# Column sums of a non-local attention block, computed from two exact halves against ones, and a group's end cut into ten pieces

## The chip, the cores and the metric

The kernel runs on one core of a Trainium2 chip. The metric is device time in microseconds (us) of one execution. Five engines run their own instruction streams in program order: PE (TensorE: weight loads and matmuls), ACT (ScalarE), DVE (VectorE), POOL (GpSimd) and SP (SyncE). Here POOL and SP mostly issue DMAs. An instruction whose operands are not ready holds up everything behind it on its engine, DMA issues included.

## The reference

```python
# x: (4, 64, 64, 256); Wq, Wk: 256 x 128; Wv: 256 x 256; N = 64 * 64
q = jnp.einsum('bwhc,cd->bwhd', x, Wq) + bq
k = jnp.einsum('bwhc,cd->bwhd', x, Wk) + bk
v = jnp.einsum('bwhc,cd->bwhd', x, Wv) + bv
pq = q.reshape(B, -1, N)
pk = k.reshape(B, -1, N)
pv = v.reshape(B, -1, N)
energy = jnp.einsum('bcn,bcm->bnm', pq, pk)
attention = jax.nn.softmax(energy, axis=-1)
out = jnp.einsum('bcm,bnm->bcn', pv, attention)
return gamma * out.reshape(B, W, H, C) + x
```

Everything is float32.

## The kernel before

**Tiling.** There are 4 images. For each, a projection stage of 16 iterations makes q, k and v; then attention runs 8 groups (g) of 512 columns n, and each group 16 steps (t) of 256 rows m. A step is counted through the image as u = 16 g + t, so an image has 128 steps. In a step the energies of two blocks of 128 rows are computed, exponentiated to a tile x of 128 x 1024, added to the running sum s, and multiplied by v into four PSUM banks a0, b0, a1, b1 (two halves of the output channels, each with a main bank a and a small-term bank b). No maximum is subtracted; a general version at the end of the program runs only if a sum leaves the safe range.

**Halves.** Matmuls take float32r operands, which keep fewer bits, so each float32 value is split: ACT multiplies it by `UPPER = 1 - 2**-13` on its way into a float32r tile (h), and DVE subtracts h from the value (l) and forms a third combination (d). `upper` and `halves` do this for x, `halve_v` for v, `project_qk` for q and k. Attention then needs three kinds of product (`attend`, line 364), the energies also three (`cross` line 307, `energy` line 322).

**Order of the work.** The schedule is written by hand: the program's order is each engine's order. Within step u PE runs the small-term energies of step u+3, the first half of the attention products of step u, the main energies of step u+2, and the second half of the products. ACT scales the small-term energies (line 308), exponentiates step u+2 (line 325) and makes its upper half (line 331). DVE works on step u+1: adds x to s (line 340), makes l (line 345) and d (line 347). In the last step of a group (t = 15) DVE also adds the two halves of s (line 351), one step ahead, and ACT empties the four banks into o (line 378).

**Buffers.** k tiles are loaded from DRAM by POOL (`load_k`, line 295), u+5 in step u; the pool `kpool` has five buffers. At the start of an image `begin` loads the tiles of steps 0 to 4 in iterations 4 to 8 of the projection stage, the q tile of group 0 in iteration 6, and computes the first energies: the small-term ones of steps 0, 1 and 2 in iterations 10, 11 and 13, the main ones of steps 0 and 1 in iterations 11 and 13. The tile f, through which q and k halves go out to DRAM on POOL's queue (kf at line 263, qd twice at line 265), has two buffers. Projection iteration i transposes x of iteration i+1 (line 122), and loads x of iteration i+2 on SP's queue (line 82; three buffers). Its four PSUM tiles in rotation are the output banks from iteration 3 on.

**A group's end.** After the last products of a group, `finish` starts; it is a Python generator, whose pieces are run one per step by `proceed`, or one per iteration of the next projection stage if the group was the image's last. Its first piece runs at once:

1. `sums`: four float32 matmuls, each with 128 columns of s (every fourth) as weights and one column of ones as moving operand, give the column sums on partitions (line 386); ACT copies 128 x 4 numbers (line 393).
2. Reciprocal (line 396); it is written to DRAM `rd` (line 398) and read back spread over all partitions as r (line 400); o's two parts are added (line 401). In the first seven groups of an image the DMAs go on SP's queue, in the last group on POOL's.
3. and 4. Nothing.
5. o times r (line 405).
6. A DMA on POOL accumulates x onto o (line 409), and o goes out (line 410).

The very last group of the program has its own end, `finish_last`.

Of the kernel before, what the change touches and what calls it, by code (L numbers as in the profile page):

```python
# [9 lines left out]
F32 = mybir.dt.float32  # L10
F32R = mybir.dt.float32r
I32 = mybir.dt.int32
AF = mybir.ActivationFunctionType
ALU = mybir.AluOpType
# [6 lines left out]
def kernel(  # L21
# [62 lines left out]

    ident = const.tile([P, P], F32, name="ident")
    make_identity(nc, ident)
    ones = const.tile([P, P], F32, name="ones")
    nc.vector.memset(ones, 1.0)
    wqk_sb = const.tile([P, KC, 2 * C2], F32, name="wqk_sb")
    bqk_sb = const.tile([P, 2 * C2], F32, name="bqk_sb")  # L90
    nc.gpsimd.dma_start(bqk_sb[:, :C2], bq.partition_broadcast(P))
# [106 lines left out]
    with ExitStack() as fast:  # L198
# [4 lines left out]
        xpool, xtpool, qkv = pool("xpool", 3), pool("xtpool", 3), pool("qkv", 1)  # L203
        ppool = pool("ppool", 2)
        work = pool("work", 2)
        kpool = pool("kpool", 5)
        dram = pool("dram", 2, space=DRAM)
        ps_e = pool("ps_e", 4, space=PSUM)
        ps_o = pool("ps_o", 1, space=PSUM)
# [2 lines left out]
        vh, vl, vd = (  # L212
            qkv.tile([P, NM, C], F32R, tag=name, name=name) for name in ("vh", "vl", "vd")
        )
        rd = dram.tile([B * NG, NB], F32, tag="rd", name="rd", bufs=1)
        nc.scalar.dma_start(wqk_sb[:, :, :C2], wq.rearrange("(k p) d -> p k d", p=P))
        nc.scalar.dma_start(wqk_sb[:, :, C2:], wk.rearrange("(k p) d -> p k d", p=P))

# [115 lines left out]
        def halves(b, u):  # L334
            if u >= STEPS:
                return
            x, h = units[b, u]
            if u % NU:
                s = now["s"]
                nc.vector.tensor_tensor(s, s, x, ALU.add)  # L340
            else:
                now["s"] = x
            ld = ppool.tile([P, 2, 2, NB], F32R, tag="ld", name=f"ld_{b}_{u}")
            l, d = ld[:, 0], ld[:, 1]
            nc.vector.tensor_tensor(l, x, h.bitcast(F32), ALU.subtract)  # L345

            nc.vector.scalar_tensor_tensor(  # L347
                d, h.bitcast(F32), 1.0 + E, x, ALU.mult, ALU.subtract
            )
            if u % NU == NU - 1:  # L350
                nc.vector.tensor_tensor(s[:, 0, :], s[:, 0, :], s[:, 1, :], ALU.add)
                now["sum"] = s[:, 0, :]
            units[b, u] = h, l, d

        def attend(b, u, j, order=(0, 1, 2)):
# [23 lines left out]
                    now["o"][:, c, j, :], now["ab"[c], j], AF.Identity, scale=scale  # L379
                )  # L380

        def sums(b, g, pool, tag):

            zp = pool.tile([P, NJ], F32, tag=tag, name=f"z_{b}_{g}")
            for j in range(NJ):
                nc.tensor.matmul(  # L386
                    zp[:, j : j + 1], now["sum"][:, j::NJ], ones[:, :1], start=True, stop=True
                )
            return zp, rall[:, b * NG + g, :]

        def finish(b, g, o):
            zp, r4 = sums(b, g, ps_o, "b0")
            nc.scalar.copy(r4, zp)
            queue = nc.sync if g < NG - 1 else nc.gpsimd
            yield
            nc.vector.reciprocal(r4, r4)
            n = b * NG + g
            queue.dma_start(rd[n : n + 1, :].rearrange("o (p j) -> (o p) j", j=NJ), r4)
            r = work.tile([P, NB], F32, tag="r", name=f"r_{b}_{g}", bufs=1)
            queue.dma_start(r, rd[n, :].partition_broadcast(P))  # L400
            nc.vector.tensor_tensor(o[:, 0], o[:, 0], o[:, 1], ALU.add)
            yield
            yield
            yield
            nc.vector.tensor_tensor(
                o[:, 0], o[:, 0], r.unsqueeze(1).to_broadcast([P, 2, NB]), ALU.mult
            )
            yield
            nc.gpsimd.dma_start(o[:, 0], xg[b, g], accum_op=ALU.add)
            queue.dma_start(og[b, g], o[:, 0])  # L410

        def inside(ok, r):

# [3 lines left out]
        def finish_last(b, u, xr):  # L417

            g = NG - 1
            attend(b, u, 0)  # L420
            zp, r4 = sums(b, g, ps_e, "e")
            nc.vector.reciprocal(r4, zp)
            work_ = ppool.tile([P, 2, NB], F32, tag="x", name="last", bufs=3)
            spread, ok = work_[:, 0].rearrange("p (q j) -> p q j", j=NJ), work_[:, 1, : B * NG * NJ]
            nc.vector.tensor_tensor(  # L425
                spread,
                ident.unsqueeze(2).to_broadcast([P, P, NJ]),
                r4.unsqueeze(1).to_broadcast([P, P, NJ]),
                ALU.mult,
            )  # L430
            inside(ok, rall.rearrange("p n j -> p (n j)"))
            nc.vector.tensor_reduce(zs, ok, AX.X, ALU.min)
            emptied(b, g, 0)
            o = now["o"]
            attend(b, u, 1, (2,))
            rp = ps_e.tile([P, NB], F32, tag="e", name="rp")
            nc.tensor.matmul(rp, ones, work_[:, 0], start=True, stop=True)  # L437
            attend(b, u, 1, (0, 1))
            np_ = ps_e.tile([P, 1], F32, tag="e", name="np")
            nc.tensor.matmul(np_, ones, zs, start=True, stop=True)  # L440
            nc.scalar.activation(o[:, 1, 1, :], now["b", 1], AF.Identity, scale=gam)
            r = work.tile([P, NB], F32, tag="r", name="r_last", bufs=1)
            nc.scalar.copy(r, rp)
            nc.vector.tensor_tensor(o[:, 0, 0, :], o[:, 0, 0, :], o[:, 1, 0, :], ALU.add)
            nc.vector.tensor_tensor(o[:, 0, 0, :], o[:, 0, 0, :], r, ALU.mult)  # L445
            nc.vector.tensor_tensor(xr[:, 0, :], xr[:, 0, :], o[:, 0, 0, :], ALU.add)  # L446
            nc.sync.dma_start(og[b, g][:, 0], xr[:, 0, :])
            nc.vector.tensor_tensor(o[:, 1, 1, :], o[:, 1, 1, :], r, ALU.mult)  # L448
            nc.vector.tensor_tensor(xr[:, 1, :], xr[:, 1, :], o[:, 1, 1, :], ALU.add)
            nc.vector.scalar_tensor_tensor(o[:, 0, 1, :], now["a", 1], gam1, r, ALU.mult, ALU.mult)  # L450
            nc.vector.tensor_tensor(xr[:, 1, :], xr[:, 1, :], o[:, 0, 1, :], ALU.add)  # L451
            nc.sync.dma_start(og[b, g][:, 1], xr[:, 1, :])
            nc.vector.tensor_scalar(again, np_, P - 0.5, None, ALU.is_lt)
# [15 lines left out]
        for b in range(B):  # L469
            pr = images[b]  # L470
            if b == 0:
                now["banks"] = energies
                pr.transposed(0)

                wp = ps_o.tile([P, P], F32, tag="b1", name="wp1")
                for _ in range(2):
                    nc.tensor.matmul(wp, ones, ones, start=True, stop=True)
                pr.transposed(1)
                project_qk(b, 0)
            for i in range(1, NI):  # L480
                if i == 3:
                    now["banks"] = outputs
                if i + 1 < NI:
                    pr.transposed(i + 1)
                begin(b, i)
                project_qk(b, i)
                if i == NI - 1:
                    halves(b, 0)
                project_v(b, i - 1)
                proceed()  # L490
            project_v(b, NI - 1)
            for u in range(STEPS):
                g, t = divmod(u, NU)
                final = (b, u) == (B - 1, STEPS - 1)
                if t == 6 and g + 1 < NG:
                    load_q(b, g + 1)
                if u == STEPS - NU and b + 1 < B:
                    image(b + 1)
                if u >= STEPS - 3 and b + 1 < B:
                    now["banks"] = energies  # L500
                    if u == STEPS - 3:
                        images[b + 1].load(0)
                    elif u == STEPS - 2:
                        images[b + 1].transposed(0)
                if (b, u) == (B - 1, STEPS - 6):
                    xr = ppool.tile([P, 2, NB], F32, tag="s", name="xr")
                    nc.sync.dma_start(xr, xg[b, g])

                beside = halve_v(b, NI - 2 + u // 4) if u in (2, 6) else iter(())
                cross(b, u + LOOK + 1)  # L510
                if not final:
                    attend(b, u, 0)
                    if t == NU - 1:
                        emptied(b, g, 0)
                energy(b, u + LOOK)
                next(beside, None)
                upper(b, u + LOOK)
                load_k(b, u + LOOK + 3)
                halves(b, u + 1)
                next(beside, None)  # L520
                if final:
                    finish_last(b, u, xr)
                    break
                attend(b, u, 1)
                if t == NU - 1:
                    emptied(b, g, 1)
                    start(finish(b, g, now["o"]))
                else:
                    proceed()
            if b + 1 < B:  # L530
                images[b + 1].transposed(1)
                project_qk(b + 1, 0)
                proceed()
# [134 lines left out]
```

## Time and profile before

| | |
|---|---|
| three runs | 2485.28, 2488.24, 2488.52 us; median 2488.24 |
| the profiled execution | 2489.29 us; its span, first to last instruction, 2487.5 us |
| mean granted TensorE clock | 0.991 |
| busy share: PE, PE weight loads, DVE, ACT, POOL | 98%, 81%, 83%, 74%, 18% |
| matmuls of line 364, 128 x 512 | 6144; mean 390 ns each, overlapping |
| matmuls of line 386 (the sums) | 256 records for 32 groups; 57.6 us busy |
| loads of k (line 295) | 512 of 384 KB; 3.4 us to landing (median) |
| accumulating DMAs (line 409) | 31 of 512 KB; 5.9 us to landing (median) |
| loads of x (line 82) | 64 of 256 KB; 4.4 us to landing (median) |

Matmuls are pipelined, so the duration of one is longer than the time from one start to the next; the time a group costs is read from start to start. A bracket behind an instruction gives the idle time of its engine just before it and what ended it. PEclk is the granted clock, 1 being full speed. POOL's "busy" is the issuing of DMAs.

### The profile page before, as it was taken

Reading aid. Unit: us, or ns where it says so; the run is one execution under the profiler, and the core shown is the slowest. Engines: PE = TensorE matmul, PEld = TensorE weight load, DVE = VectorE, ACT = ScalarE, POOL = GpSimd, SP = SyncE. Lnnn points to the kernel's source line nnn. Section 1 sums busy time; section 2 is a strip of 40 time slices with the busy share of each in tenths; the row PEclk is TensorE's granted clock in tenths of the full one; section 3 lists DMA queues with packets and bytes.
Section 4 is the critical chain, followed back from the end, with each engine's and each line's share of the span. In section 5 each row is a group of like instructions: output and inputs, shape, how many; then the busy total and the mean of one; then the engine's idle time right before and its main releaser. Section 6 shows DMA issues by size and latency. Waiting matters only on the chain. (4 is left out here: it accounts for less than half of the span.)

```text
span 2487.5 us, 30812 instructions
## 1 busy us (share of the span) xinstructions
PE 2428.3 (98%) x10774; PEld 2022.1 (81%) x10774; DVE 2055.8 (83%) x2027; ACT 1832.0 (74%) x3040; POOL 435.6 (18%) x790
## 2 busy tenths in 40 slices
PE   9999999999799999999989999999998999999998
PEld 7788888888688888888868888888886788888886
DVE  5888888888588888888768888888876888888887
ACT  4777777777477777777657777777765777777775
POOL 3211111110321111111032111111113211111110
PEclk9999999999999999999999999999999999999999
DMA  8544444443854444444385444444438444444442
GB/s 250 155 127 127 106 119 131 127 126 95 243 159 126 127 110 114 134 128 121 97 254 153 129 126 127 109 115 135 127 93 257 145 129 130 129 120 118 111 133 74
DMA packets 149779, 338.11 MB, mean 136 GB/s; under 512 B 18641, under 2 KB 51921, under 8 KB 149617
## 3 DMA queue, kind: packets, MB, share of 16 engines
q0 software_dynamic: 115424, 295.89, 42.3%
q1 hardware_dynamic: 33648, 39.91, 5.5%
q8 instruction: 88, 1.44, 0.2%
q14 instruction: 75, 0.61, 0.1%
q10 hardware_dynamic: 544, 0.26, 0.0%
HBM read 268.83 MB, written 67.17 MB: 135 GB/s over the span
## 5 line engine op out<-in xcount | busy, mean ns | idle before, releaser
L325 ACT ACTIVATE x<-e 128x512 f32<-128x512 f32 x960 | 522.3, 597 | 431.3 <-PE e L322 431.2
L340 DVE TENSOR_TENSOR s<-s,x 128x1024 f32<-128x1024 f32 x480 | 587.9, 1225 | 243.9 <-ACT x L325 239.8
L364 PE MATMUL a<-ld,vl 128*128 128x512 f32 x2048 | 631.8, 390 | 6.9 <-DVE ld L345 6.9
L364 PE MATMUL b<-ld,vd 128*128 128x512 f32 x2048 | 632.6, 390 | 1.7 <-DVE ld L347 1.6
L364 PE MATMUL a<-h,vh 128*128 128x512 f32 x2048 | 632.4, 390 | 0.5 <-ACT v L165 0.5
L345 DVE TENSOR_TENSOR ld<-x,h 128x1024 fp32r<-128x1024 f32 x480 | 585.3, 1219 | 2.8 <-DMA qd<-f 2.8
L347 DVE SCALAR_TENSOR_TENSOR ld<-h,x 128x1024 fp32r<-128x1024 f32 x480 | 585.0, 1219 | 0.0
L295 POOL DMA_DIRECT2D k<-kf x512 | 284.2, 556 | 1580.9 <-PE e L322 1456.8
L322 PE MATMUL e<-q,k 128*128 128x512 f32 x2048 | 550.9, 391 | 0.5 <-ACT e L308 0.4
L308 ACT ACTIVATE e<-e 128x512 f32<-128x512 f32 x1024 | 545.0, 566 | 5.0 <-PE e L307 4.9
L331 ACT ACTIVATE h<-x 128x1024 fp32r<-128x1024 f32 x480 | 509.4, 1061 | 15.0
L364 PEld LDWEIGHTS a<-ld,vl 128*128 128x128 f32 x2048 | 384.4, 188 | 88.8 <-DVE ld L345 8.6
L364 PEld LDWEIGHTS b<-ld,vd 128*128 128x128 f32 x2048 | 384.5, 188 | 83.7 <-issue 2.6
L322 PEld LDWEIGHTS e<-q,k 128*128 128x128 f32 x2048 | 385.1, 188 | 81.8 <-ACT e L308 1.5
L364 PEld LDWEIGHTS a<-h,vh 128*128 128x128 f32 x2048 | 384.6, 188 | 81.5 <-ACT v L165 1.2
L307 PE MATMUL e<-q,k 128*128 128x512 f32 x1024 | 319.4, 393 | 0.0
L307 PEld LDWEIGHTS e<-q,k 128*128 128x128 f32 x1024 | 190.6, 189 | 37.4
L260 DVE SCALAR_TENSOR_TENSOR f<-f,qks 128x512 fp32r<-128x512 f32 x128 | 82.8, 689 | 95.3 <-ACT f L258 95.3
L258 ACT ACTIVATE f<-qks 128x512 fp32r<-128x512 f32 x64 | 40.4, 632 | 136.0 <-DVE qks L144 68.6
L135 PE MATMUL qk<-wqk_sb,xts 128*128 128x256 f32 x512 | 131.8, 403 | 3.3 <-ACT xts L128 3.2
L156 PE MATMUL v<-xts,wv_sb 128*128 128x256 f32 x512 | 121.6, 382 | 1.5 <-DVE qks L144 1.5
L135 PEld LDWEIGHTS qk<-wqk_sb,xts 128*128 128x128 f32 x512 | 99.4, 202 | 20.3 <-ACT xts L128 6.5
(67 smaller groups left out, 1093.7 us busy)
## 6 DMA issues: line engine op xcount, KB each, us to landing
k<-kf POOLq DMA_DIRECT2D x512, 384.0 KB, 3.4
kf<-f POOLq DMA_DIRECT2D x64, 384.0 KB, 3.1
qd<-f POOLq DMA_DIRECT2D x128, 192.0 KB, 3.8
q<-qd POOLq DMA_DIRECT2D x32, 768.0 KB, 7.9
x<-in_x_dram SPq DMA_DIRECT2D x64, 256.0 KB, 4.4
o<-in_x_dram POOLq DMA_DIRECT2D x31, 512.0 KB, 5.9
out_dram<-o SPq DMA_DIRECT2D x28, 512.0 KB, 5.5
r<-rd SPq DMA_DIRECT2D x28, 256.0 KB, 4.5
```

What stands on the lines that cost most here:

```text
L135: nc.tensor.matmul(qk[:, s, :], self.xt[i][:, k, s, :], wqk_sb[:, k, :], start=(k == 0), stop=(k == KC - 1),)
L156: nc.tensor.matmul(vp[:, eh, :], wv_sb[:, k, eh * P : (eh + 1) * P], self.xt[i][:, k].rearrange("p s a -> p (s a)"), start=(k == 0), stop= ...
L295: nc.gpsimd.dma_start(t, kf[b, u % NU])
L307: nc.tensor.matmul(e, *forms(b, u, i, 2), start=True, stop=False, skip_group_check=True)
L308: nc.scalar.mul(e, e, -1.0 / (1.0 + E))
L322: nc.tensor.matmul(e, *forms(b, u, i, f), start=False, stop=(f == 1), skip_group_check=True)
L325: nc.scalar.activation(x[:, i, :], e, AF.Exp, scale=(1.0 + E) / E)
L331: nc.scalar.activation(h, units[b, u], AF.Identity, scale=UPPER)
L340: nc.vector.tensor_tensor(s, s, x, ALU.add)
L345: nc.vector.tensor_tensor(l, x, h.bitcast(F32), ALU.subtract)
L347: nc.vector.scalar_tensor_tensor(d, h.bitcast(F32), 1.0 + E, x, ALU.mult, ALU.subtract)
L364: nc.tensor.matmul(to, (vh, vl, vd)[f][:, t + NU * i, j * P : (j + 1) * P], units[b, u][f][:, i, :], start=(t == 0 and i == 0 and f != 1), ...
```

## The change

The sums become two float32r matmuls with a matrix of ones as weights: they stream the upper half and the remainder of s, 512 columns each, and put the column sums on every partition of bank b0. The two halves are made in the group's last step by a new generator, `sum_forms`, one ACT and one DVE instruction, placed between the others of the step. They take the buffer of r, which doubles in size, and `kpool` goes from five buffers to four. The row of sums (one partition) is copied by ACT into the old s tile, written to DRAM `zd`, and read back spread as 128 x 4; from there on the reciprocal, `rd` and r are as before. Each DMA that depends on the one before it is issued a step later, so `finish` has ten pieces: sums and copy; zd written; zd read; reciprocal, rd written and o's parts added; r read; nothing; o times r; accumulation; nothing; output. All DMAs but the accumulation go on SP's queue, in the last group of an image too. The ones are made on DVE from the identity matrix instead of by a memset. The last group of the program keeps its four float32 matmuls.

```diff
-    ones = const.tile([P, P], F32, name="ones")
-    nc.vector.memset(ones, 1.0)
+    ones_r = const.tile([P, P], F32R, name="ones")
+    ones = ones_r.bitcast(F32)
+    nc.vector.tensor_scalar(ones_r, ident, 0.0, 1.0, ALU.mult, ALU.add)
...
-        kpool = pool("kpool", 5)
+        kpool = pool("kpool", 4)
...
-        rd = dram.tile([B * NG, NB], F32, tag="rd", name="rd", bufs=1)
+        zd, rd = (dram.tile([B * NG, NB], F32, tag=n, name=n, bufs=1) for n in ("zd", "rd"))
...
-                now["sum"] = s[:, 0, :]
+                now["sum"] = s
...
-        def sums(b, g, pool, tag):
...
-        def finish(b, g, o):
-            zp, r4 = sums(b, g, ps_o, "b0")
-            nc.scalar.copy(r4, zp)
-            queue = nc.sync if g < NG - 1 else nc.gpsimd
+        def sum_forms(b, g):
+
+            s = now["sum"]
+            f = work.tile([P, 2, NB], F32R, tag="r", name=f"zf_{b}_{g}", bufs=1)
+            h, l = now["z"] = f[:, 0, :], f[:, 1, :]
+            nc.scalar.activation(h, s[:, 0, :], AF.Identity, scale=UPPER)
+            yield
+            nc.vector.tensor_tensor(l, s[:, 0, :], h.bitcast(F32), ALU.subtract)
+            yield
+
+        def finish(b, g, o, s):
+            n = b * NG + g
+            r4 = rall[:, n, :]
+            row = lambda t: t[n : n + 1, :]
+            spread = lambda t: row(t).rearrange("o (p j) -> (o p) j", j=NJ)
+            zp = ps_o.tile([P, NB], F32, tag="b0", name=f"z_{b}_{g}")
+            for f, x in enumerate(now["z"]):
+                nc.tensor.matmul(zp, ones_r, x, start=(f == 0), stop=(f == 1))
+            nc.scalar.copy(s[0:1, 0, :], zp[0:1, :])
+            yield
+            nc.sync.dma_start(row(zd), s[0:1, 0, :])
+            yield
+            nc.sync.dma_start(r4, spread(zd))
             yield
             nc.vector.reciprocal(r4, r4)
-            n = b * NG + g
-            queue.dma_start(rd[n : n + 1, :].rearrange("o (p j) -> (o p) j", j=NJ), r4)
+            nc.sync.dma_start(spread(rd), r4)
+            nc.vector.tensor_tensor(o[:, 0], o[:, 0], o[:, 1], ALU.add)
+            yield
             r = work.tile([P, NB], F32, tag="r", name=f"r_{b}_{g}", bufs=1)
-            queue.dma_start(r, rd[n, :].partition_broadcast(P))
-            nc.vector.tensor_tensor(o[:, 0], o[:, 0], o[:, 1], ALU.add)
-            yield
+            nc.sync.dma_start(r, rd[n, :].partition_broadcast(P))
             yield
             yield
...
             nc.gpsimd.dma_start(o[:, 0], xg[b, g], accum_op=ALU.add)
-            queue.dma_start(og[b, g], o[:, 0])
+            yield
+            yield
+            nc.sync.dma_start(og[b, g], o[:, 0])
...
-                beside = halve_v(b, NI - 2 + u // 4) if u in (2, 6) else iter(())
+                beside = iter(())
+                if u in (2, 6):
+                    beside = halve_v(b, NI - 2 + u // 4)
+                elif t == NU - 1 and not final:
+                    beside = sum_forms(b, g)
+                    total = now["sum"]
```

More of the change, by code (lines that the diff above doesn't have):

```diff
@@ L380, in emptied @@
                 )
-        def sums(b, g, pool, tag):
[L384 to L389, printed above, removed]
-        def finish(b, g, o):
-            zp, r4 = sums(b, g, ps_o, "b0")
-            nc.scalar.copy(r4, zp)
-            queue = nc.sync if g < NG - 1 else nc.gpsimd
+        def sum_forms(b, g):
[19 more added lines that the diff above has]
+            nc.sync.dma_start(r4, spread(zd))
             yield
             nc.vector.reciprocal(r4, r4)
-            n = b * NG + g
-            queue.dma_start(rd[n : n + 1, :].rearrange("o (p j) -> (o p) j", j=NJ), r4)
-            r = work.tile([P, NB], F32, tag="r", name=f"r_{b}_{g}", bufs=1)
-            queue.dma_start(r, rd[n, :].partition_broadcast(P))
+            nc.sync.dma_start(spread(rd), r4)
             nc.vector.tensor_tensor(o[:, 0], o[:, 0], o[:, 1], ALU.add)
             yield
+            r = work.tile([P, NB], F32, tag="r", name=f"r_{b}_{g}", bufs=1)
+            nc.sync.dma_start(r, rd[n, :].partition_broadcast(P))
             yield
@@ L420, in finish_last @@
             attend(b, u, 0)
-            zp, r4 = sums(b, g, ps_e, "e")
+            zp = ps_e.tile([P, NJ], F32, tag="e", name="zp")
+            for j in range(NJ):
+                nc.tensor.matmul(
+                    zp[:, j : j + 1], now["sum"][:, 0, j::NJ], ones[:, :1], start=True, stop=True
+                )
+            r4 = rall[:, B * NG - 1, :]
             nc.vector.reciprocal(r4, zp)
@@ L526 @@
                     emptied(b, g, 1)
-                    start(finish(b, g, now["o"]))
+                    start(finish(b, g, now["o"], total))
                 else:
```

## The prediction

> **What bounds the kernel now.** I read the page first, then the groups by shape, the PE timeline of one group end, the four projection stages, and the waits of POOL and SP.
>
> ```profile
> PE 2428.3 (98%) x10774; PEld 2022.1 (81%) x10774; DVE 2055.8 (83%) x2027; ACT 1832.0 (74%) x3040; POOL 435.6 (18%) x790
> L386 PE MATMUL z<-ones,s 128*128 128x1 f32 x256 | 57.6, 346 | 0.0
> ```
>
> TensorE sets the pace. In a steady step it starts 18 matmuls in 4.08 us (0.227 each), while ACT has 3.4 us and DVE 3.7 us of work in the step. The sums z are 256 records, of which 248 belong to the 31 groups that change. One group end, PE and then ACT:
>
> ```profile
> 2408.40 1.80 PE L386 MATMUL z<-ones,s 128*128 128x1 f32 x8
> 2410.06 0.70 PE L307 MATMUL e<-q,k 128*128 128x512 f32 x2
> 2411.53 0.62 PE L364 MATMUL b<-ld,vd 128*128 128x512 f32 x2
> ...
> 2407.03 1.09 ACT L325 ACTIVATE x<-e 128x512 f32<-128x512 f32 x2
> 2408.15 1.06 ACT L331 ACTIVATE h<-x 128x1024 fp32r<-128x1024 f32 x1
> 2409.68 0.68 ACT L378 ACTIVATE o<-b,gam 128x512 f32<-128x512 f32 x1
> 2410.25 0.16 ACT L393 COPY rall<-z 128x4 f32<-128x4 f32 x1
> ```
>
> PE never idles here: z takes 1.66 us, and a group is 67.07 us where 16 steps are 65.28. ACT is late: it runs without a break from 2404.8, because the four emptyings of the outputs (2.7 us) fall into this step.
>
> The other cost lies in the projection stages. Windows of images 0 to 3 that end at the first attention matmul (those of 1 to 3 start 2.2 us of matmuls earlier in the program; columns: stretch, its length, busy time by engine, clock, DMA share, GB/s):
>
> ```profile
> 12.30:81.20 68.90, 66.16 (x322) 57.43 (x321) 48.68 (x91) 42.84 (x86) 27.03 (x51) 0.98 0.82 250
> 620.30:703.90 83.60, 71.04 (x334) 59.60 (x334) 51.43 (x95) 44.07 (x89) 29.93 (x55) 0.94 0.76 227
> 1241.20:1321.20 80.00, 69.91 (x333) 58.74 (x333) 51.87 (x95) 44.23 (x89) 29.97 (x55) 0.96 0.80 238
> 1858.30:1938.30 80.00, 69.91 (x333) 59.10 (x334) 51.66 (x95) 44.02 (x89) 29.94 (x55) 0.96 0.81 238
> ```
>
> From the same instruction on (the transposition of iteration 1) image 0 takes 68.9 us and the others, less 2.2, take 81.4, 77.8 and 77.8: 30.3 us more in all, and only the others carry a finish of the image before. Its stalls, POOL, ACT and PE of image 1 and then PE of image 0:
>
> ```profile
> 658.99 0.72 POOL L410 DMA_DIRECT2D out_dram<-o  x1 [5.57 <-DMA o<-in_x_dram]
> 667.08 0.63 ACT L258 ACTIVATE f<-qks 128x512 fp32r<-128x512 f32 x1 [9.37 <-DMA qd<-f]
> 668.49 1.11 PE L122 MATMUL xt<-ident,x 128*128 128x128 f32 x4 [6.83 <-ACT v L165]
> ...
> 51.15 0.81 PE L122 MATMUL xt<-ident,x 128*128 128x128 f32 x4 [2.74 <-ACT v L165]
> ```
>
> POOL waits for the accumulating DMA before it may issue the output; kf and qd queue behind it; ACT cannot refill f (two buffers); PE gets no free bank. After both idles PE runs at a granted clock of 0.5: one stretch of 3.4 us (cost about 1.7) after the idle of 2.74, one of 6.8 us (about 2.6 over the next matmuls) after 6.83.
>
> **The change, part by part.** *Sums in mid-image (28 groups).* Four fp32 matmuls become two of 512 columns at 0.227 each: if nothing waited, 1.79 - 0.45 = 1.34 us per group. But their operands come late. The activation for the upper half stands behind the exponentials, so it starts at 2408.15 and ends 0.63 later (row L258, same shape) at 2408.78; DVE subtracts in 0.69 (row L351, 512 wide), 2409.47, and waits for nothing else (its step ended at 2407.3). PE, free at 2408.40, starts the second sum at 2409.52 and the next step at 2409.75 instead of 2410.06. ACT then owes h and two emptyings, all 0.54 later, until 2410.76, and copies the sum out of bank b0. One partition of 512 has no row; between 0.16 (four elements) and 0.59 (512) I take 0.58, since length and not partitions separates these rows: 2411.34. PE wants b0 six matmuls after 2409.75, at 2411.11, and waits to 2411.40, where it was at 2411.53 before. So 0.13 us per group is left of 1.34, with bounds of -0.3 and +0.5: **-3.6 us** for 28. The finish after it (sum to DRAM and back, reciprocal at step 2, multiply at step 5, accumulation at 6, output at 8) has no reader on PE, and o is reused only at step 15: nothing. Of the three groups that end an image, the sums wait less, 0.5 gained each: **-1.5**.
>
> *kpool 5 to 4, steady.* The load of k for step u+5 now waits for energy(u+1), one step later. That leaves 3 x 4.08 - 3.2 = 9.0 us to its reader; loads land in 3.4 (median), at worst 8.7 in the stretch with q and the accumulation. Hidden, cover 0.3 us at the worst.
>
> *kpool at the start of an image.* Iterations 4 to 8 still load five k tiles before anything reads one. The fifth now needs the buffer of the first, which energy(0) frees in iteration 11, and POOL issues in order:
>
> ```profile
> POOL k L295 <- PE e L322: 1456.8, 422, 5.3
> SPq L410 <- DMA o<-in_x_dram: 537.7, 28, 20.6
> ```
>
> Queued behind it are kf and qd of iterations 8 to 10; f of iteration 10 (ACT) needs those of 8 out. In image 0 energy(0) ended at 58.6. Then k, kf and two qd issue, 0.53 each; kf and qd alone land 3.85 after the first issue (rows at 61.8), with k ahead about 1.5 more: f at 64.1, v of iteration 9 empties at 65.5, and the transposition that stood at 62.48 goes at 65.5. That is 3.1 idle and 1.7 of half clock: **+4.8 us** in image 0, 4.5 in each later one, where I find 2.8 idle. The Trainium skill (TensorE: Matmul & The Clock Gate, "HAM oscillation") warns of idle gaps over about 3.4 us only. By that rule the four half clocks here would fall away, 6.8 us less; the row with 2.74 idle and a half clock after it speaks against it.
>
> *The finish of a finished image, now all on SP.* POOL loses its waits, and SP gets them, among the loads of x: zd, x3, r4, x4, rd, x5, r, x6 to x10, output, x11. Two of them bite.
> (a) rd waits for the reciprocal, which DVE reaches only after f of iteration 2 and the halves of v: counted from the first transposition of image 1 (620.3), DVE ends them at 633.5; rd goes out, x5 is issued at 634.0 and lands 4.4 later (its median). PE wants it at 634.2: 4.2 idle and 1.7 of half clock, **5.9**.
> (b) The output waits for the accumulation, issued in iteration 6 behind q, kf and qd. On image 0's clock q was issued at 37.5 and landed after 9.3, the last qd of iteration 6 landed at 49.5, and accumulations land about 4.2 after the qd before them (4.4, 4.3, 3.5 in images 2, 3, 1): 53.7. Then the output and, 0.54 behind, x11; its landing under load lies between 3.0 and 9.6, I take 5.5: 59.9. PE got there at 51.15 in image 0, so 8.8 more, and 0.9 more of half clock: **9.7**.
> A later stage is then 68.9 - 0.8 (image 0 starts it at half clock) + 5.9 + 9.7 + 4.5 = 88.2 us; three of them 264.6 against 237.0 now: **+27.6 us**. The POOL stalls are gone and bigger ones stand in their place. Bounds for one stage: 72.6 (x5 and x11 in time, k as above) to 97 (both landing in 9.6).
>
> *Ones from the identity.* The warm-up matmuls start at about 2.6 instead of 1.05 and end by 8.0; the second transposition waits for x until 7.94 anyway: 0, at most +1.5.
>
> **Sum.** -3.6 - 1.5 + 4.8 + 27.6 = +27.3 us. The profiled execution took 2489.29 (span 2487.5 and 1.8 around it), 1.05 above the median of 2488.24; on that median: 2515.5, said as 2515. About 0.2% (5 us) is what a measurement of this kernel can tell from no change.
>
> **Rivals.** *The image changes get cheaper.* If SP's waits end before PE needs x (the point: x11 landed by 51 on image 0's clock, x5 by 634), a later stage is image 0's with the late k, 68.1 + 4.5 = 72.6, three are 19.2 us shorter than now, and the sum is -3.6 - 1.5 + 4.8 - 19.2 = -19.5: 2469. For it: waits on POOL of 18.9 and 12.7 us go. Against: line SPq L410 shows SP standing for the accumulation, and x11 cannot pass it. Chance 0.15.
> *The sums come free.* If the halves are ready when the attention matmuls end, 1.34 x 28 = 37.5 instead of 3.6 is saved: 2481. Against: ACT runs without a gap from 2404.8 to 2410.4, and the new activation stands in that row. Chance 0.06.
> *The short stalls gate the clock.* The group end holds about 1.1 us of idle within 3 us. At 703.9 to 706.1 idles of 1.5 and 0.4 were followed by a half clock at 706.9; at 1876 one of 1.85 was not. If half of the 28 ends lose 1.7 us, +24: 2539. Chance 0.12.
> *The errors cancel* (the output lands early, x5 late): within 5 us of now, 0.05.
>
> **How the numbers follow.** The forecast, slower by the waits moved onto SP and by the fifth k, has 0.62; its own range is 2496 to 2534 (5 us either way in each of the three stages, 4 in the groups). Faster is the cheap changes and nearly all of the free sums, 0.2; same is the cancelling errors and the rest of the free sums, 0.06; slower is the forecast and the gated clock, 0.74. The range 2474 to 2545 cuts the far half of the cheap image changes and the top of the gated clock.
>
> **What would show it.** Right: PE idle before the transpositions of iterations 4 and 10 in images 1 to 3, released by DMA x; POOL k waiting for PE e in every projection stage, image 0's about 74 us; mid-image groups at about 66.9 us, PE idle at the sums, released by DVE and ACT. Wrong: later stages under 78 us, or groups at 65.7.

## The result and the profile after

The changed kernel is slower: 2504.18 us median against 2486.76 for the kernel before, a ratio of 1.0074 (95% interval 1.0053 to 1.0095). The profiled executions took 2508.35 and 2489.29 us, 19.1 apart. 2515 was forecast, inside a range of 2474 to 2545.

The page's first part, after:

```profile
PE 2417.9 (96%) x10588; PEld 1980.8 (79%) x10588; DVE 2072.6 (83%) x2058; ACT 1854.0 (74%) x3071; POOL 429.2 (17%) x781
```

PE does 10 us less work, in a span 19 us longer: the loss is waiting. Where it waits is in the four projection stages, shown as windows from the same instructions as before (stretch, length, busy time by engine, clock, DMA share, GB/s). In these four windows PE's idle time goes from about 35 to 57 us, and its busy time from 277 to 288, because matmuls at half clock take longer:

```profile
9.90:85.30 75.40, 68.45 (x322) 58.23 (x321) 49.45 (x92) 43.44 (x87) 27.47 (x53) 0.93 0.78 235
622.10:713.20 91.10, 73.65 (x334) 62.41 (x333) 52.04 (x95) 45.08 (x90) 28.09 (x52) 0.89 0.73 212
1247.40:1338.40 91.00, 73.57 (x333) 62.11 (x331) 52.38 (x96) 45.70 (x92) 28.12 (x52) 0.89 0.72 213
1871.90:1959.60 87.70, 72.66 (x333) 61.77 (x332) 51.73 (x95) 44.84 (x90) 28.13 (x52) 0.88 0.74 220
```

68.9, 83.6, 80.0 and 80.0 us have become 75.4, 91.1, 91.0 and 87.7, at a granted clock of 0.88 to 0.93 instead of 0.94 to 0.98, and the DMA engines are less busy, not more. The PE timeline of image 1 has three large gaps (start, duration, instruction, and in brackets the idle time before it and what ended it):

```profile
642.00 1.12 PE L123 MATMUL xt<-ident,x 128*128 128x128 f32 x4 [5.92 <-DMA x<-in_x_dram]
...
674.77 1.08 PE L123 MATMUL xt<-ident,x 128*128 128x128 f32 x4 [6.12 <-DMA x<-in_x_dram]
...
691.52 1.12 PE L123 MATMUL xt<-ident,x 128*128 128x128 f32 x4 [4.40 <-ACT v L166]
```

These are the transpositions of iterations 4, 10 and 12. The first two wait for x. SP's timeline shows why:

```profile
636.84 0.33 SPq L408 DMA_DIRECT2D rd<-rall  x1
637.26 0.55 SPq L82 DMA_DIRECT2D x<-in_x_dram  x1
641.51 0.32 SPq L412 DMA_DIRECT2D r<-rd  x1
...
668.67 0.59 SPq L422 DMA_DIRECT2D out_dram<-o  x1
669.36 13.51 SPq L82 DMA_DIRECT2D x<-in_x_dram  x5
```

Each load of x leaves right behind a DMA that had to wait: rd for the reciprocal (DVE at 636.64), the output for the accumulation (issued at 661.84, landed 6.8 us later). The third gap starts on POOL and reaches PE through ACT (one line of each timeline):

```profile
683.51 0.53 POOL L296 DMA_DIRECT2D k<-kf  x1 [17.62 <-PE e L308]
```

```profile
690.11 0.63 ACT L259 ACTIVATE f<-qks 128x512 fp32r<-128x512 f32 x1 [12.66 <-DMA qd<-f]
```

POOL stands for 17.6 us before the fifth k load. In image 0 it is 12.8 us. Its buffer is that of the image's first k tile, which PE frees with the first main energies in iteration 11.

A group's end, PE and then ACT, against that of before:

```profile
2429.10 0.61 PE L365 MATMUL b<-ld,vd 128*128 128x512 f32 x2
2429.84 0.49 PE L400 MATMUL z<-zf,ones 128*128 128x512 f32 x1
2430.57 0.50 PE L400 MATMUL z<-zf,ones 128*128 128x512 f32 x1 [0.23 <-DVE zf L390]
2430.90 0.61 PE L308 MATMUL e<-q,k 128*128 128x512 f32 x2
...
2432.36 0.73 PE L365 MATMUL b<-ld,vd 128*128 128x512 f32 x2
```

```profile
2429.14 0.65 ACT L388 ACTIVATE zf<-s 128x512 fp32r<-128x512 f32 x1
2429.66 1.08 ACT L332 ACTIVATE h<-x 128x1024 fp32r<-128x1024 f32 x1
2430.61 0.71 ACT L379 ACTIVATE o<-a,gam 128x512 f32<-128x512 f32 x1
2431.18 0.72 ACT L379 ACTIVATE o<-b,gam 128x512 f32<-128x512 f32 x1
2431.75 0.56 ACT L401 COPY s<-z 1x512 f32<-1x512 f32 x1
```

The products end at about 2429.55. The first sum starts 0.3 us later, when zf is there, the second 0.7 after that, behind DVE's subtraction; then b0 opens when the copy has ended (2432.31), and the matmul into it starts at 2432.36. From first sum to first sum a group is 66.87 us on average (781.00 to 847.89 in image 1), where it was 67.07.

### The profile page after: what moved, and what is told of

Read it like the earlier page. It is cut to its first block, busy times and chain, and to the rows that moved or that the text cites. A ratio compares the mean times of both kernels' runs of the same rounds, so it can differ in the third digit from the quotient of the medians.

```text
span 2506.6 us, 30467 instructions
## 1 busy us (share of the span) xinstructions
PE 2417.9 (96%) x10588; PEld 1980.8 (79%) x10588; DVE 2072.6 (83%) x2058; ACT 1854.0 (74%) x3071; POOL 429.2 (17%) x781
## 4 chain that ended last, share of the span: by engine, by line
PE 83%; ACT 6%; issue 4%; DMA 4%; DVE 3%; POOL 1%; SPq 0%; DVEq 0%; ACTq 0%; POOLq 0%
PE a L365 36%; PE b L365 18%; PE e L323 17%; PE e L308 9%; DMA qd<-f 2%; ACT o L379 2%; PE qk L136 1%; ACT v L166 1%; DVE zf L390 1%; ACT x L326 1%; PE v L157 1%; DMA x<-in_x_dram 1%; ACT f L259 1%; ACT zf L388 1%; ACT vh L279 1%
## 5 line engine op out<-in xcount | busy, mean ns | idle before, releaser
L296 POOL DMA_DIRECT2D k<-kf x512 | 273.7, 535 | 1765.9 <-PE e L323 1584.8
L365 PEld LDWEIGHTS a<-h,vh 128*128 128x128 f32 x2048 | 384.7, 188 | 81.4 <-ACT v L166 1.0
L136 PE MATMUL qk<-wqk_sb,xts 128*128 128x256 f32 x512 | 138.5, 419 | 0.1
L136 PEld LDWEIGHTS qk<-wqk_sb,xts 128*128 128x128 f32 x512 | 104.9, 213 | 17.6 <-ACT xts L129 2.1
```

Source lines behind the costliest of these rows:

```text
L136: nc.tensor.matmul(qk[:, s, :], self.xt[i][:, k, s, :], wqk_sb[:, k, :], start=(k == 0), stop=(k == KC - 1),)
L296: nc.gpsimd.dma_start(t, kf[b, u % NU])
L365: nc.tensor.matmul(to, (vh, vl, vd)[f][:, t + NU * i, j * P : (j + 1) * P], units[b, u][f][:, i, :], start=(t == 0 and i == 0 and f != 1), ...
```

## The experiments

The theory after the result: three waits, each at the head of an in-order queue, make the projection stages long, and the new sums are worth little because two waits in a row hold the group's end. The rivals: the longer way over DRAM costs by its traffic wherever it is placed, or one wait covers the other. The stages below are counted from the transposition of iteration 1 to the first attention matmul; before they were 68.9, 81.4, 78.4 and 77.9 us (the last 0.5 of image 2's lies behind its window), in the changed kernel 75.4, 89.0, 88.8 and 85.6.

### The fifth k load after its buffer is free (e1_k_late)

```diff
-            if i in (4, 5, 6, 7, 8):
-                load_k(b, i - 4)
+            if i in (4, 5, 6, 7, 12):
+                load_k(b, min(i - 4, 4))
```

> The changed kernel, but the fifth k tile of an image is loaded in iteration 12 of the projection stage, after energy(0) in iteration 11 has freed its buffer, instead of in iteration 8. Theory (the fifth k load blocks POOL's queue, and through kf, qd and f the matmuls): the idle of about 4.3 us before the transposition of iteration 12 and the 6.8 us of half clock after it go in all four projection stages, about 6.9 us each; image 0's stage from the transposition of iteration 1 to attention goes from 75.4 to about 68.5, the others from 89, 89, 86 to about 82, 82, 79; total near 2477. Rival (the stalls of x stand ahead of it and would cover it in images 1 to 3): only image 0 gains, total near 2497.

Measured: 2481.67 us, ratio to the kernel before 0.9987 (0.9977 to 0.9996). The stages are 67.8, 81.9, 82.3 and 81.1 us. The idle before iteration 12 is gone in all four. So this one load alone decides whether the change is 0.7% slower than the kernel before or 0.1% faster, level with it for practical purposes, and the rival that had it hidden in images 1 to 3 falls. One thing came back: the gap before iteration 10 grew, on the PE timeline of image 1 from 6.1 to 8.6.

```profile
665.76 1.09 PE L123 MATMUL xt<-ident,x 128*128 128x128 f32 x4 [8.61 <-DMA x<-in_x_dram]
```

Its x landed 6.7 us after its issue instead of 5.3. That the kf and qd writes, no longer held back by POOL, took the bandwidth is likely, and not shown. The total stayed 5 us above the 2477 that were expected.

### The output of an image's last group three iterations later (e2_out_late)

```diff
+            gap = (0, 1, 2, 1, 5) if g == NG - 1 else (0, 1, 2, 1, 2)
...
             nc.gpsimd.dma_start(o[:, 0], xg[b, g], accum_op=ALU.add)
-            yield
-            yield
+            for _ in range(gap[4]):
+                yield
             nc.sync.dma_start(og[b, g], o[:, 0])
```

> The changed kernel, but in a group that ends an image the output is issued three pieces later (iteration 11 instead of 8). Theory (the output on SP's queue waits for the accumulation and holds up the load of x for iteration 10): the idle of 6 us before the transposition of iteration 10 and its half clock go, about 8 us in each of three stages, less what f's wait leaves (2.7 idle in image 0): stages near 82, total near 2487 to 2492. Rival (x is late because of the traffic of q, kf, qd and the accumulation, not because of its place in the queue): idle before iteration 10 stays within 1 us, total 2504.

Measured: 2492.37 us, ratio 1.0032 (1.0019 to 1.0046); stages 75.0, 83.0, 82.6 and 82.4. The accumulation is where it was, but iteration 10 no longer waits for x (PE, images 1 and 2):

```profile
666.48 0.66 PE L123 MATMUL xt<-ident,x 128*128 128x128 f32 x4 [0.86 <-ACT v L166]
...
1285.23 0.66 PE L123 MATMUL xt<-ident,x 128*128 128x128 f32 x4 [1.51 <-ACT v L166]
```

In image 1 that x is now issued at 654.41, ahead of the accumulation (658.98), instead of behind its landing. The x after it, issued at 658.30 into the same traffic, took 7.8 us to land, and no matmul waited for it either. So the place in the queue cost the time, not the traffic of q, kf, qd and the accumulation. The output's own 512 KB moved along with the edit and were not separated.

### rd and r spaced (e3_rd_late)

The same loop with `gap = (1, 2, 1, 1, 2)` for the image's last group: one piece between the reciprocal and rd, two from rd to r, one from r to the multiply; o's parts are added just before r.

> The changed kernel, but in a group that ends an image rd is written one piece after the reciprocal, r is read two pieces after that and the multiply comes one piece after r; accumulation and output follow as before, one iteration later. Theory (rd waits on SP for the reciprocal and r for rd, and the loads of x behind them come late): the idle of 4 to 6 us before the transposition of iteration 4, its half clock and the small idle of iteration 5 go, 7 to 9 us in each of three stages, while the idle before iteration 10 moves to iteration 11 with its size; total near 2480. Rival (the longer way over DRAM costs wherever it is placed): no stage shorter by more than 2 us, total 2500 to 2506.

Measured: 2484.91 us, ratio 0.9998 (0.9987 to 1.0008); stages 75.3, 80.0, 79.6 and 78.6, so 9.0, 9.2 and 7.0 less. Iteration 4 waits no longer. Iteration 5 still does, for 2.4, 0.7 and 0.5 us, where the changed kernel had 1.0, 0.7 and none: this small idle did not go, as was expected, and grew in image 1. The gap at iteration 10 moved to iteration 11, with 4.0 to 4.4 us, not its full size, so a part of the saving belongs to the output's wait (PE, image 1):

```profile
642.62 1.08 PE L123 MATMUL xt<-ident,x 128*128 128x128 f32 x4 [2.36 <-DMA x<-in_x_dram]
...
673.17 1.09 PE L123 MATMUL xt<-ident,x 128*128 128x128 f32 x4 [4.02 <-DMA x<-in_x_dram]
```

### Four k buffers in the kernel before (e4_four_k_alone)

```diff
-        kpool = pool("kpool", 5)
+        kpool = pool("kpool", 4)
```

> The kernel before with kpool of four buffers instead of five and nothing else. Theory: POOL waits for energy(0) at the fifth k load in every projection stage and the matmuls stall at iteration 12: plus 4 to 7 us in image 0 and 4 to 7 in each later stage, total 2505 to 2515, that is at least as slow as the whole change; in the steps of attention nothing (4.08 us each, groups 67.07). Rival (the loads of k one step later also cost in the steps): groups over 67.3 us, total over 2520. Second rival (in images 1 to 3 the stalls of POOL's own finish cover it): only image 0 loses, total near 2493.

Measured: 2513.52 us, ratio 1.0105 (1.0085 to 1.0124): by the middle values more than the whole change costs, though the two intervals overlap a little. Attention of image 0 starts at 85.81 instead of 81.19, and the later stages are 87.6, 86.5 and 84.1, 6.2 to 8.2 longer. Groups stay at 67.07. POOL's line in image 1:

```profile
685.80 0.53 POOL L295 DMA_DIRECT2D k<-kf  x1 [11.01 <-PE e L307]
```

Both rivals fall: nothing is lost in the steps, and POOL's own waits for the finish do not cover it. By the middle values the rest of the change is a small gain, some 8 us (1.0074 against 1.0105); since the intervals overlap, its size is not shown.

### All three at once (e5_all_late)

The late k load, and `gap = (1, 2, 2, 1, 5)`.

> The changed kernel with the fifth k tile loaded in iteration 12, and in a group that ends an image rd one piece after the reciprocal, r two pieces after rd, accumulation in iteration 8 and the output five pieces after it. Theory (three waits in queues make the projection stages long, and nothing else of the change does): no wait of the matmuls for x in images 1 to 3, their stages from the transposition of iteration 1 to attention near image 0's 68, at most 72 with the traffic of the accumulation; 82 minus 70 is 12 us in each of three stages against the run with the late k alone: total 2440 to 2450. Rival (a longer finish costs by its traffic): stages over 76, total over 2462.

Measured: 2452.57 us, ratio 0.9867 (0.9852 to 0.9882); stages 68.2, 70.2, 70.9 and 69.4. The total is 3 us over the expectation, the stages are in it. The finish still takes its way over DRAM, and a later stage takes only 1.2 to 2.7 us more than image 0's. What its traffic costs is not separated by this, since image 0 alone has an idle at iteration 10 (3.0 us, and 3.4 us at half clock after it). PE's waits for x are not all gone, as was expected, but down to one in each later image, of 1.78, 1.60 and 0.41 us.

Alone, the three edits gave 22.5 (e1), 11.8 (e2) and 19.3 us (e3) against the changed kernel, 53.6 together, and all at once 51.6. So the three waits hardly cover one another.

### The halves made at the head of the step (e6_sums_early)

```diff
+                if t == NU - 1:
+                    next(beside, None)
+                    next(beside, None)
                 cross(b, u + LOOK + 1)
```

> The changed kernel, but the two halves of the running sum are made at the head of a group's last step, ahead of the other ACT and DVE work of the step. Theory (two waits in a row bind a group's end: the sums for their halves, then bank b0 for the copy that ACT reaches only after emptying a1 and b1): the wait before the sums goes, but the b0 wait grows by as much, since ACT has the same work before the copy; groups stay within 0.15 us of 66.88, total within 5 us of 2504. Rival (the halves alone bind): groups about 66.1 to 66.3, total 2482 to 2488.

Measured: 2503.08 us, ratio 1.0074 (1.0059 to 1.0089): no gain. The sums now follow the products at once, and the time reappears at b0 (PE):

```profile
286.57 0.62 PE L400 MATMUL z<-zf,ones 128*128 128x512 f32 x2
...
289.46 0.73 PE L365 MATMUL b<-ld,vd 128*128 128x512 f32 x2 [0.88 <-ACT s L401]
```

In the list of waits, weight loads for b behind the copy go from 9.9 to 36.6 us in all. Groups are 66.94 to 66.98 us, 0.08 longer than in the changed kernel.

### And the copy ahead of the emptying (e7_early_copy_first)

```diff
-                    emptied(b, g, 1)
                     start(finish(b, g, now["o"], total))
+                    emptied(b, g, 1)
```

> As the run before, and the sums' copy stands on ACT ahead of the emptying of a1 and b1. Theory: both waits go; the sums follow the attention matmuls and b0 is free before it is wanted; groups 65.8 to 66.2 us (two matmuls of 0.227 over 16 steps of 4.08 give 65.73), 0.7 to 1.0 us less in each of 28 groups, total 2476 to 2485. Rival (emptying a1 and b1 0.5 us later makes the second half of the products wait): groups 66.5 or more.

Measured: 2475.75 us, ratio 0.9957 (0.9942 to 0.9973); groups 65.93 to 65.98, 1.1 us less than before. In the list of waits the one for the copy is down to this:

```profile
PEld b L365 <- ACT s L401: 4.5, 28, 0.2
```

### Everything together (e8_all)

> All edits of the other runs together: late k, spaced finish at an image's end, early halves, copy first. If the stages and the group ends are separate costs, the savings add: about 2445 minus 20 to 25 us, total 2418 to 2428, 2.3 to 2.7 percent less than the kernel before.

Measured: 2424.67 us, ratio 0.9749 (0.9736 to 0.9763), so 2.5% faster than the kernel before. The two kinds of saving add: 51.6 us below the changed kernel by the stages (e5), 28.4 by the group ends (e7), 79.5 by both. The windows of its four stages:

```profile
10.50:78.50 68.00, 65.75 (x322) 56.66 (x321) 49.48 (x92) 43.47 (x87) 27.25 (x52) 0.97 0.86 261
605.50:680.60 75.10, 68.34 (x333) 56.79 (x331) 51.32 (x95) 45.47 (x91) 28.20 (x52) 1.00 0.86 256
1209.10:1282.40 73.30, 67.79 (x333) 56.87 (x331) 51.91 (x95) 46.17 (x93) 28.22 (x52) 1.00 0.86 264
1810.20:1881.70 71.50, 67.44 (x334) 57.07 (x333) 50.61 (x93) 44.31 (x88) 28.20 (x52) 1.00 0.88 263
```

## Why the prediction was right, and where its terms were off

The direction, the three queues and their places were right; the sum was 8 us too high (by the medians 10: 17.4 us measured), and of the three terms of a later stage none had its right size. They cancelled: 3.3 too little, 5.5 too much and 3.0 too little, by the figures below for image 1. That the total came so near is luck.

| part | forecast | measured in the profiled runs |
|---|---|---|
| three image changes, last product to first product | +26.1 (27.6 - 1.5) | 86.58, 83.59, 83.09 to 93.54, 93.66, 90.37: +24.3 |
| start of attention in image 0 | +4.8 | 81.19 to 85.29: +4.1 |
| the four attention stretches | -3.6 | -7.5, of which 28 groups at 0.20: -5.7 |
| after the last product loop | 0 | -1.8 |
| sum | +27.3 | +19.1 |

The last product is counted from the start of the image's last half step. What shortened the attention stretches by the remaining 1.8 us, and the program's end by 1.8, was not traced. The prediction's window of image 2 ended 0.5 us early, so its +27.6 should have been some 0.6 less. Its loads of k "at worst 8.7" reach 8.95 in the steps; e4 shows that nothing is lost there all the same.

**x behind rd.** Forecast 5.9, measured 9.2 in image 1: iteration 5 began at 648.99, that much after an undisturbed one would have (3.89 us an iteration). The reciprocal ran 14.6 us after the first transposition, not 13.2, because f of iteration 2 waited 3.0 us for the first qd; and I let a stretch of 3.4 us at half clock follow where one of 6.8 came.

**x behind the output.** Counted from an undisturbed iteration 10 (48.1 on image 0's clock) I had 11.8 of delay (53.7, 0.54 and 5.5 make 59.7, not 59.9) and 2.6 of half clock, 14.4; measured 6.3 and 2.6, 8.9. The failed step is the accumulation's landing, carried over from image 0's clock as 13.4 us after the transposition of iteration 8: it came after 8.0. q landed in 7.2 us instead of 9.3, and the accumulation soon behind it, probably because the gap at iteration 4 had let the transfers drain (that was not tried by itself). A row from a stage without the first stall was used for a stage that has it.

**The fifth k.** Forecast 4.5 to 4.8 per stage, measured 7.5 in image 1 (4.6 of delay, 3.0 of half clock). In e1 image 0's stage is 7.6 shorter, 1.6 of it before iteration 11, where the idle at iteration 10 was shorter and no half clock followed. The wait itself was as worked out in kind, through kf, qd, f and v; the idle is 4.2 to 4.5 in place of 2.8 to 3.1, and 6.8 us at half clock followed it in every image, not 3.4.

**The rule of the Trainium skill.** "HAM oscillation" (the Trainium skill, TensorE: Matmul & The Clock Gate) warns of idle gaps over about 3.4 us. By it the four half clocks after the fifth k would have fallen away, 6.8 us less, since I took these idles for shorter; I kept them because of the row with 2.74 us of idle. The idles came out longer than its limit, so they do not test it. But image 0 after again has 2.64 us of idle at iteration 10 and then a half clock of 3.4 us, although 2.64 is under that limit.

**The sums.** Forecast 0.13 saved per group, measured 0.20, by the two waits named. e6 and e7 show that both are needed to explain it: without the first wait 66.95, without both 65.95, where two matmuls over 16 steps of 4.08 make 65.73. The copy moved ahead alone, with the late halves, was not run.

**The rivals.** Cheaper image changes fell with the SP lines above; e5 shows what they would have been worth. The free sums fell with the groups of 66.87 us; e7 comes near them. The clock at the group ends never fell to half: the trace has the low clock only in the four stages, just behind them and at the program's end, and the groups are alike to 0.03 us.

**Ones from the identity.** I put 0 with a bound of +1.5, and it was a gain: the transposition of iteration 1 started at 9.90 instead of 12.26. Image 0's stage is therefore 6.5 longer, while attention starts only 4.1 later; that this is near the forecast 4.8 is luck too.

## What to carry to other kernels

A DMA that is issued a step later still blocks its queue if what it waits for takes longer than a step; ask of each moved DMA when its dependency lands, and what stands behind it. A buffer that is taken away from a pool has to be counted where the pool is filled in advance, not only where it turns over: here the steps lost nothing and the prologue lost all. A faster instruction at the end of a stretch brings little until the next holder of the same bank is early too: here 0.20 of 1.34 us, and 1.12 with both waits gone.

## What was not expected of the hardware

The copy of one partition of 512 elements took ACT 0.56 us, as long as the copies of 128 partitions of 512 (0.57), so that alone was as assumed.

What was not assumed is when the clock falls. In all ten traces the granted clock changes only at points that lie a multiple of 3.41 us apart; where the first of them falls differs from run to run. With PE's idle time, as the profile shows it, counted in each stretch between two such points (the last 20 us of each program left out):

- After a stretch at full clock with more than 2.01 us of idle, the next was at half clock (77 of 77). With 1.4 to 2.0 us of idle both came. With less, the next was always at full clock.
- After a stretch at half clock with 0.71 us of idle or more, the next was at half clock again (46 of 46); with 0.62 us or less, it was at full clock (98 of 98).

So the length of a gap alone does not decide its cost. In the changed kernel the idles of 4.2 to 6.1 us were followed by 6.8 us at half clock, the one of 2.64 us by 3.4. But in e6 an idle of 5.17 us (image 1, iteration 4) was followed by only 3.4 us, and one of 2.83 us in image 0 by none: it lay across such a point, with 1.76 us before it and 1.06 behind.

And warm-up matmuls that start later can be worth more. Before, they ran from 1.05, PE then idled 1.48 us for x (0.68 and 0.80 us in two stretches), and the projections ran at half rate until about 14; after, they ran from 2.67 without an idle behind them, and the projections had full rate from 8.18 (PE, changed kernel):

```profile
2.67 3.36 PE L197 MATMUL wp<-ones 128*128 128x128 f32 x14 [2.67 <-DVE ones L89]
6.14 1.09 PE L123 MATMUL xt<-ident,x 128*128 128x128 f32 x4
...
8.18 1.89 PE L136 MATMUL qk<-wqk_sb,xts 128*128 128x256 f32 x8
```

The first projection of q and k takes 1.89 us here and took 3.62 before. The transposition of iteration 1 starts at 9.6 to 10.5 us in all eight kernels with the later warm-up, and at 12.3 and 11.7 in the two without (before and e4). No run changes the warm-up alone.
